# One zero-separated running sum for numerator and denominator, and shared instructions for the first two tiles, in a bidirectional decay scan

## The chip, the cores and the metric

The kernel runs on one core of a Trainium2 chip. The metric is device time in microseconds (us) of one launch. The core has a matrix engine (TensorE, shown as PE, with PEld for its weight loads), a vector engine (VectorE, DVE), a scalar engine for functions such as exp and ln (ScalarE, ACT), a general engine (GpSimd, POOL) and a queue for transfers (SyncE, SP). Each engine works through its own instruction list in order.

## The reference

The input is 32 images of 192 channels and 56 x 56 pixels in float32. Four blocks follow each other, each as `x = x + block(groupnorm(x))`: an attention block, a scan block, a block of shifts, and a long convolution. Only the second is touched. It takes the 3136 pixels of an image as a sequence of tokens, and per channel:

```
k = Wk x;  v = Wv x;  r = Wr x          (192 x 192 products per token)
decay = exp(-exp(w_decay))
p[t+1] = decay * p[t] + exp(k[t]) * v[t]     numerator
q[t+1] = decay * q[t] + exp(k[t])            denominator
y[t]   = (p[t] + exp(u) exp(k[t]) v[t]) / (q[t] + exp(u) exp(k[t]))
x_bi   = 0.5 * (y forwards + y backwards in time)
h      = layernorm over channels( sigmoid(r) * x_bi )
block  = Wo h
```

The reference writes the recurrence with a running maximum; the kernel computes the plain sums above and keeps records by which a guarded version can take over where exponents are large.

## The kernel before, in words

The scan block is `scan_pairs`. It handles two images at a time (16 pairs). A pair is held as three tiles of 128 partitions: tile 0 has channels 0 to 127 of the first image, tile 1 those of the second, tile 2 channels 128 to 191 of both. Time is cut into NM = 4 chunks of MC = 784 tokens, so an operand is 128 x 784. `turned()` gives a PSUM tile of two banks; there are four.

For each chunk there are three pieces of work:

- `forwards(s, m)` (L1170): normalise x on ACT (L1141); for tiles 0 and 1 together, then for tile 2, multiply by Wk, take exp on ACT into `both[:, 1]` (L1183), multiply by Wv, and multiply by the exponential on DVE into `both[:, 0]` (L1188). So `both` holds numerator terms in its first row and denominator terms in its second. Then, per tile, `scan` (L1144) runs one DVE scan per row (L1153), with the carried value `at` as its start and the decay read as a broadcast scalar; POOL puts the carry in the edge column of the result `pq` before (L1150) and takes the new carry from its other end after (L1156); one DVE instruction over 2 x 784 adds the token's own term (L1157). ACT inverts the denominator by Ln and Exp (L1161, L1162), and DVE multiplies into y (L1198).
- `backwards(s, m)` (L1200): the same scan with time reversed over the kept `both`, then the multiply by the inverse (L1220), the addition to the forward y (L1221) and the multiply by the gate g (L1222), where g is a sigmoid in three ACT instructions (L1212 to L1217).
- `finish(s, m)` (L1225): the layer norm and Wo. PE centres (`centre`), ACT squares (L1237), PE averages (`mean_w`), ACT makes the reciprocal deviation `rd` (L1246, L1247), PE multiplies by Wo, and DVE scales from PSUM (L1260) and adds the residual (L1263). ACT's squares for the next norm (L1270) are put off into the following `forwards`.

The loop at L1298 goes through the pairs. For each of the four steps i it emits the first part of `backwards` for chunk 3 - i, the first part of `finish` for the chunk before, then the second parts of both, and then `forwards` for chunk i of the next pair. The next pair's chunk 3 is the last to go forwards and the first to go backwards.

Nobody writes the engines' orders by hand. The program order above sets priorities, and at build time a scheduler places each instruction on its engine's list when its inputs, and a free buffer of its tile's tag, are there by its own reckoning. On the chip the lists are fixed. Buffers: 12 of `both`, 16 of y, 3 of `pq`, 9 of the tag `t` (g, sq, rd), 7 of x.

Of the kernel before, what the change touches and what calls it, by code (L numbers as in the profile page):

```python
# [20 lines left out]
F32 = mybir.dt.float32  # L21
I32 = mybir.dt.int32
AF = mybir.ActivationFunctionType
ALU = mybir.AluOpType
# [12 lines left out]
MC = 784  # L37
NM = N // MC
# [899 lines left out]
def scan_pairs(ctx: ExitStack, tc: tile.TileContext, a, k, x1, st_a, st_c, x2, rs2, count):  # L938
# [5 lines left out]
    nc = tc.nc  # L944
    NB = x1.shape[0]
    cp = ctx.enter_context(tc.tile_pool(name="s_c", bufs=1))
    kp = ctx.enter_context(tc.tile_pool(name="s_k", bufs=3 * NM))
    wp = ctx.enter_context(tc.tile_pool(name="s_w", bufs=9))
    sp = ctx.enter_context(tc.tile_pool(name="s_s", bufs=2))
    pp = ctx.enter_context(tc.tile_pool(name="s_p", bufs=4, space=PSUM))  # L950
    pairs = _Pairs(nc)
# [1 line left out]
    def small(name, shape):  # L953
        return cp.tile(shape, F32, name=name, tag=name)
# [19 lines left out]
    wk, wv, wr = (_blocks_of(weights, 448 * i) for i in range(3))  # L974
# [7 lines left out]
    cb = small("cb", [128, 2])  # L982
    ps, _, _ = turned()
# [15 lines left out]
    eu = small("eu", [128, 2])  # L999
# [31 lines left out]
    def of(t):  # L1031
        return slice(0, 1) if t < 2 else slice(1, 2)
# [93 lines left out]
    class State:  # L1126


        def __init__(self, p):
            self.p = p  # L1130
            self.seen = sp.tile([128, 5, 3 * NM], F32, name="seen", tag="seen", bufs=3)
            self.both, self.y = {}, {}
# [8 lines left out]
            nc.scalar.activation(xs[t], xs[t], AF.Identity, bias=nb1[:, t, s.p : s.p + 1], scale=rs1[:, t, s.p : s.p + 1])  # L1141
        return [parts(t) for t in xs]

    def scan(s, m, t, carry, rev):  # L1144

        both, at = s.both[m][t], carry[t]
        z = wp.tile([128, 2, MC + 1], F32, name="pq", tag="pq", bufs=3)
        edge, last = (MC, 0) if rev else (0, MC)
        out, before = (z[:, :, 0:MC], z[:, :, 1:]) if rev else (z[:, :, 1:], z[:, :, 0:MC])
        nc.gpsimd.tensor_copy(z[:, :, edge], at)  # L1150
        for i in range(2):
            to, data = (out[:, i, ::-1], both[:, i, ::-1]) if rev else (out[:, i], both[:, i])
            nc.vector.tensor_tensor_scan(  # L1153
                to, decay[:, of(t)].to_broadcast([128, MC]), data, at[:, i : i + 1], ALU.mult, ALU.add
            )
        nc.gpsimd.tensor_copy(at, z[:, :, last])  # L1156
        nc.vector.scalar_tensor_tensor(before, both, eu[:, of(t)], before, ALU.mult, ALU.add)  # L1157
        return before[:, 0], before[:, 1]

    def inverse(s, den, m, t, which):  # L1160
        nc.scalar.activation(den, den, AF.Ln)  # L1161
        nc.scalar.activation(den, den, AF.Exp, scale=-1.0, accum_out=s.seen[:, which, 3 * m + t : 3 * m + t + 1])  # L1162

    def start(way):
        carry = [sp.tile([128, 2], F32, name=f"{way}{t}", tag=f"{way}{t}") for t in range(3)]
        for c in carry:
            nc.gpsimd.memset(c, 0.0)  # L1167
        return carry

    def forwards(s, m, behind=()):  # L1170
        s.both[m] = [kp.tile([128, 2, MC], F32, name="both", tag="both") for _ in range(3)]
        s.y[m] = [kp.tile([128, MC], F32, name="y", tag="y", bufs=3 * NM + 4) for _ in range(3)]
        xn = normed(s, m)
        for tiles in ((0, 1), (2,)):
            for wt in (wk, wv):
                ps = [turned() for _ in tiles]
                if len(tiles) == 2:
                    pairs.outer(wt, [q[2] for q in ps], xn)
                else:
                    pairs.inner(wt, ps[0][2], xn)  # L1180
                for t, (_, both, _) in zip(tiles, ps):
                    if wt is wk:
                        nc.scalar.activation(  # L1183
                            s.both[m][t][:, 1].rearrange("p (h n) -> p h n", h=2), both, AF.Exp,
                            accum_out=s.seen[:, 0, 3 * m + t : 3 * m + t + 1],
                        )
                    else:
                        nc.vector.tensor_tensor(  # L1188
                            s.both[m][t][:, 0].rearrange("p (h n) -> p h n", h=2), both,
                            s.both[m][t][:, 1].rearrange("p (h n) -> p h n", h=2), ALU.mult,  # L1190
                        )
                if wt is wk and tiles == (0, 1):
                    for later in behind:
                        later()
            for t in tiles:
                num, den = scan(s, m, t, s.fore, False)
                inverse(s, den, m, t, 1)
                nc.vector.tensor_tensor(s.y[m][t], num, den, ALU.mult)  # L1198

    def backwards(s, m):  # L1200

        xn = normed(s, m)
        h = s.y[m]
        for tiles in ((0, 1), (2,)):
# [5 lines left out]
            for t, (_, both, _) in zip(tiles, ps):  # L1210
                g = wp.tile([128, MC], F32, name="g", tag="t")
                nc.scalar.activation(  # L1212
                    g.rearrange("p (h n) -> p h n", h=2), both, AF.Exp, scale=-1.0,
                    accum_out=s.seen[:, 3, 3 * m + t : 3 * m + t + 1],
                )
                nc.scalar.activation(g, g, AF.Ln, bias=1.0)
                nc.scalar.activation(g, g, AF.Exp, scale=-1.0)  # L1217
                num, den = scan(s, m, t, s.back, True)
                inverse(s, den, m, t, 2)
                nc.vector.tensor_tensor(num, num, den, ALU.mult)  # L1220
                nc.vector.tensor_tensor(h[t], h[t], num, ALU.add)  # L1221
                nc.vector.tensor_tensor(h[t], h[t], g, ALU.mult)  # L1222
            yield

    def finish(s, m):  # L1225

        h, xs = s.y[m], load(s.p, m)
        hs = [parts(t) for t in h]
        sq = [wp.tile([128, MC], F32, name="sq", tag="t") for _ in range(3)]
        for tiles in ((0, 1), (2,)):  # L1230
            ps = [turned() for _ in tiles]
# [4 lines left out]
            for t, (_, both, _) in zip(tiles, ps):  # L1236
                nc.scalar.activation(  # L1237
                    sq[t].rearrange("p (h n) -> p h n", h=2), both, AF.Square,
                    accum_out=s.seen[:, 4, 3 * m + t : 3 * m + t + 1],
# [4 lines left out]
        rds = [wp.tile([128, MC], F32, name="rd", tag="t") for _ in range(3)]  # L1244
# [8 lines left out]
        for tiles in ((0, 1), (2,)):  # L1253
            po = [turned() for _ in tiles]
            if len(tiles) == 2:
                pairs.outer(wog, [q[2] for q in po], hs)
            else:
                pairs.inner(wog, po[0][2], hs)
            for t, (_, out, _) in zip(tiles, po):
                nc.vector.tensor_tensor(  # L1260
                    sq[t].rearrange("p (h n) -> p h n", h=2), out, rds[t].rearrange("p (h n) -> p h n", h=2), ALU.mult
                )
                nc.vector.scalar_tensor_tensor(  # L1263
                    xs[t], sq[t], cb[:, of(t)], xs[t], ALU.add, ALU.add, accum_out=s.sums[:, t, m : m + 1]
                )
                if m == NM - 1:
                    nc.vector.tensor_scalar(s.away[:, t], s.sums[:, t, m : m + 1], -1.0 / MC, None, ALU.mult)

                def square(t=t):
                    nc.scalar.activation(  # L1270
                        sq[t], xs[t], AF.Square, bias=s.away[:, t], accum_out=s.squares[:, t, m : m + 1]
                    )

                left.append(square)
# [20 lines left out]
    s, before = State(0), None  # L1295
    for m in range(NM):
        forwards(s, m)
    for p in range(NP):  # L1298
        ahead = State(p + 1) if p + 1 < NP else None
        for i in range(NM):  # L1300
            m = NM - 1 - i
# [20 lines left out]
        before, s = s, ahead  # L1322
# [20 lines left out]
    ps, _, _ = turned()  # L1343
# [642 lines left out]
```

## Time and profile before

| | us |
|---|---|
| three runs, median (lowest to highest) | 10588.62 (10584.67 to 10590.73) |
| the profiled execution: its time | 10570.28 |
| its span in the profile | 10568.5 |
| DVE busy in the whole span | 9096.0 |
| PE busy in the whole span | 9496.5 |
| ACT busy, POOL busy | 6336.3, 2212.1 |
| granted TensorE clock | 0.96 of full |

The profile's rows name line, engine, operation, output and inputs with the shape of one instruction, how often it ran, its total and mean duration, and the idle time of its engine just before it with what ended it. Mean durations of DVE instructions overlap: the next one starts before the last has ended, so the distance between two starts in the timeline is less than the duration. The four blocks follow one another, and the scan block lies between about 4800 us and 8060 us of the span. In the timeline, the same order of instructions comes back every four chunks, 204.3 us apart.

### The profile page before, as it was taken

Reading aid. Unit: us, or ns where it says so; the run is one execution under the profiler, and the core shown is the slowest. Engines: PE = TensorE matmul, PEld = TensorE weight load, DVE = VectorE, ACT = ScalarE, POOL = GpSimd, SP = SyncE. Lnnn points to the kernel's source line nnn. Section 1 sums busy time; section 2 is a strip of 40 time slices with the busy share of each in tenths; the row PEclk is TensorE's granted clock in tenths of the full one; section 3 lists DMA queues with packets and bytes.
Section 4 is the critical chain, followed back from the end, with each engine's and each line's share of the span. In section 5 each row is a group of like instructions: output and inputs, shape, how many; then the busy total and the mean of one; then the engine's idle time right before and its main releaser. Section 6 shows DMA issues by size and latency. Waiting matters only on the chain. (4 is left out here: it accounts for less than half of the span.)

```text
span 10568.5 us, 164015 instructions
## 1 busy us (share of the span) xinstructions
PE 9496.5 (90%) x64134; PEld 5888.6 (56%) x64134; DVE 9096.0 (86%) x11284; ACT 6336.3 (60%) x11964; POOL 2212.1 (21%) x1750
## 2 busy tenths in 40 slices
PE   5999999999999999998888888888888789999998
PEld 3555555555555655554334433334433677777786
DVE  5888888888888888887999999999999577878787
ACT  3555555555555555554666666666666466767676
POOL 0000000000000000001333333333333444444441
PEclk9999999999999999999899999999999899999999
DMA  4211222112221111102344443444444588989898
GB/s 126 67 53 48 66 67 67 49 52 67 67 67 46 55 48 48 48 27 63 90 102 106 104 99 99 106 102 107 103 99 105 169 271 272 283 274 283 271 279 268
DMA packets 1111104, 1247.70 MB, mean 118 GB/s; under 512 B 773092, under 2 KB 813441, under 8 KB 1098233
## 3 DMA queue, kind: packets, MB, share of 16 engines
q1 hardware_dynamic: 1089388, 1209.08, 39.8%
q10 hardware_dynamic: 20932, 28.02, 1.0%
q8 instruction: 510, 8.36, 0.3%
q14 instruction: 274, 2.24, 0.1%
HBM read 916.15 MB, written 306.43 MB: 116 GB/s over the span
## 5 line engine op out<-in xcount | busy, mean ns | idle before, releaser
L649 DVE SCALAR_TENSOR_TENSOR o<-v_a,att_w,o 128x896 f32<-128x896 f32 (+1 forms) x1024 | 1057.2, 1032 | 421.7 <-ACT v_a L623 301.8
L1167 POOL MEMSET f<- 128x2 f32 x48 | 4.5, 99 | 4744.0 <-DMA st_c<-st 4741.5
L1546 DVE STREAM_TRANSPOSE z<-turned 128x1792 f32<-128x1792 f32 x192 | 677.5, 3529 | 273.2 <-ACT turned L1546 272.9
L1546 ACT COPY y<-ps 64x252 f32<-64x252 f32 (+1 forms) x2304 | 782.1, 339 | 155.1 <-PE ps L1546 125.6
L1161 ACT ACTIVATE pq<-pq 128x784 f32<-128x784 f32 x384 | 329.3, 858 | 679.9 <-DVE pq L1157 679.9
L1153 DVE TENSOR_TENSOR_SCAN pq<-decay,f,both 128x784 f32<-128x784 f32 x384 | 695.5, 1840 | 9.0 <-ACT both L1183 9.0
L1157 DVE SCALAR_TENSOR_TENSOR pq<-both,eu,pq 128x1568 f32<-128x1568 f32 x384 | 701.3, 1840 | 2.0 <-POOL f L1156 0.4
L666 ACT ACTIVATE pr<-ps,low 98x896 f32<-98x896 f32 (+1 forms) x384 | 352.0, 917 | 573.4 <-DVE low L664 573.4
L1153 DVE TENSOR_TENSOR_SCAN pq<-decay,b,both 128x784 f32<-128x784 f32 x384 | 694.1, 1839 | 0.0
L921 PE MATMUL ps<-x,weights 128*128 128x392 f32 x1536 | 587.1, 521 | 93.2 <-ACT x L1141 60.8
L649 DVE SCALAR_TENSOR_TENSOR o<-v_c,att_w,o 128x448 f32<-128x448 f32 (+1 forms) x1024 | 638.6, 624 | 4.8
L662 PE MATMUL ps<-xs_a,gk_a 128*98 128x448 f32 (+1 forms) x1536 | 636.6, 495 | 0.0
L663 PE MATMUL ps<-xs_c,gk_c 125*98 125x448 f32 (+1 forms) x1536 | 631.3, 492 | 0.0
L776 ACT ACTIVATE pq<-pq 128x1176 f32<-128x1176 f32 (+2 forms) x224 | 241.9, 1080 | 640.6 <-DVE pq L768 618.6
L1141 ACT ACTIVATE x<-x,nb,rs 128x784 f32<-128x784 f32 x384 | 386.6, 1030 | 334.3 <-DMA x<-x 178.2
L763 PE MATMUL ps<-gq_a,xs_a 128*128 128x294 f32 (+1 forms) x1600 | 547.0, 425 | 37.8 <-DVE pq L768 33.1
L1546 POOL TENSOR_TENSOR xn<-x,scale 128x896 f32<-128x896 f32 x192 | 334.9, 1744 | 1171.5 <-DMA x<-x 684.2
L1546 PEld LDWEIGHTS ps<-toep,y 128*32 128x32 f32 x16896 | 515.8, 151 | 113.4 <-ACT y L1546 110.6
L1546 PE MATMUL ps<-toep,y 128*32 128x112 f32 x16896 | 563.0, 291 | 0.0
L1156 POOL COPY b<-pq 128x2 f32<-128x2 f32 x192 | 405.4, 2111 | 660.8 <-DVE pq L1153 567.6
L764 PE MATMUL ps<-gq_c,xs_c 125*128 125x294 f32 (+1 forms) x1600 | 520.1, 413 | 0.0
L1546 ACT ACTIVATE turned<-ps,rs 128x448 f32<-128x448 f32 (+1 forms) x576 | 383.3, 666 | 212.8 <-PE ps L1546 206.3
(360 smaller groups left out, 23569.4 us busy)
## 6 DMA issues: line engine op xcount, KB each, us to landing
toep<-spans SPq DMA_DIRECT2D x192, 2352.0 KB
x<-x SPq DMA_DIRECT2D x576, 392.0 KB
x<-x SPq DMA_DIRECT2D x896, 196.0 KB
out_x<-done SPq DMA_DIRECT2D x384, 196.0 KB
spans<-lags SPq DMA_DIRECT2D x24, 2352.0 KB
x<-in_x SPq DMA_DIRECT2D x32, 1568.0 KB
x<-x SPq DMA_DIRECT2D x32, 1568.0 KB
gq_c<-once SPq DMA_DIRECT2D x32, 821.1 KB
```

The lines of the kernel that those rows point to most:

```text
L649: nc.vector.scalar_tensor_tensor(dst, tap(i), dww[:, t, i : i + 1], dst, ALU.mult, ALU.add)
L662: mm(ps[P2, h, :n], g[:, cols], xs_a[j][:, px], start=True, stop=False)
L663: mm(ps[P2, h, :n], gk_c[0:KC, 2 * j + h, cols], xs_c[j][0:KC, px], start=False, stop=True)
L666: nc.scalar.activation(pr[:, :, :n], ps[P2, :, :n], AF.Exp, bias=low[:, j, p : p + 1], accum_out=sums[:, j, p : p + 1])
L763: mm(ps[:m, k - q, :HA], xs_a[j][:, px], g, start=True, stop=False)
L764: mm(ps[:m, k - q, :HA], xs_c[j][0:KC, px], gq_c[0:KC, which[k]], start=False, stop=True)
L921: mm(out, aa, srcs[t][h], start=True, stop=False)
L1141: nc.scalar.activation(xs[t], xs[t], AF.Identity, bias=nb1[:, t, s.p : s.p + 1], scale=rs1[:, t, s.p : s.p + 1])
L1153: nc.vector.tensor_tensor_scan(to, decay[:, of(t)].to_broadcast([128, MC]), data, at[:, i : i + 1], ALU.mult, ALU.add)
L1156: nc.gpsimd.tensor_copy(at, z[:, :, last])
L1157: nc.vector.scalar_tensor_tensor(before, both, eu[:, of(t)], before, ALU.mult, ALU.add)
L1546: return lambda *args, **kw: self.tc.keep_in_program_order(do(*args, **kw))
```

## The change

Only `scan_pairs` is changed. Its edits:

- **One scan per tile.** `both` gets a column in front of each row and one behind the last: numerator and denominator of a tile lie behind each other as [edge, 784, edge, 784, edge]. POOL copies the carries into the edge columns (in front of the rows, or behind them when time is reversed). One DVE scan runs over 2 x 785 elements from 0.0. Its factors come from a new constant `factors`, which is zero at the place of each edge column and the decay elsewhere, so that at an edge the sum restarts from the carry.
- **Sets.** Tiles 0 and 1 become one set that shares `both`, `pq`, the carry, y and g; tile 2 is the other. Own terms (before L1157), Ln and Exp of the denominators, the gate's Ln and Exp, and the DVE products (L1198, L1220 to L1222) are one instruction for both tiles of a set. The scan stays one per tile, and so do the instructions that read PSUM.
- **In-place writes.** Backwards, own terms are added into `both`, not into `pq`; in `finish`, rd is overwritten, not sq.
- **Buffers.** `both`: 4 per set; y: 5 per set; `pq`: 1 per set; g of the first set: 1; tag `t`: 4.
- POOL clears the record `seen` at the start of each pair, since shared instructions leave some of its columns unwritten.

```diff
-    kp = ctx.enter_context(tc.tile_pool(name="s_k", bufs=3 * NM))
-    wp = ctx.enter_context(tc.tile_pool(name="s_w", bufs=9))
+    kp = ctx.enter_context(tc.tile_pool(name="s_k", bufs=NM))
+    wp = ctx.enter_context(tc.tile_pool(name="s_w", bufs=4))
...
+    factors = small("factors", [128, 2, 2 * (MC + 1)])
+    for i in range(2):
+        of_i = factors[:, i].rearrange("p (n c) -> p n c", n=2)
+        nc.vector.memset(of_i[:, :, 0:1], 0.0)
+        nc.vector.tensor_copy(of_i[:, :, 1:], decay[:, i : i + 1].unsqueeze(2).to_broadcast([128, 2, MC]))
...
+    SETS = ((0, 1), (2,))
+
+    def scan(s, m, i, carry, rev):
+
+        both, at = s.both[m][i], carry[i]
+        n, kind = at.shape[1], of(SETS[i][0])
+        z = wp.tile([128, n, MC + 1], F32, name="pq", tag=f"pq{n}", bufs=1)
+        last = 0 if rev else MC
+        nc.gpsimd.tensor_copy(both[:, rev * (MC + 1) :: MC + 1][:, :n], at)
+        for k in range(0, n, 2):
+            to = z[:, k : k + 2].rearrange("p n c -> p (n c)")
+            data = both[:, rev + k * (MC + 1) : rev + (k + 2) * (MC + 1)]
+            if rev:
+                to, data = to[:, ::-1], data[:, ::-1]
+            nc.vector.tensor_tensor_scan(to, factors[:, kind.start], data, 0.0, ALU.mult, ALU.add)
         nc.gpsimd.tensor_copy(at, z[:, :, last])
-        nc.vector.scalar_tensor_tensor(before, both, eu[:, of(t)], before, ALU.mult, ALU.add)
-        return before[:, 0], before[:, 1]
+        own, others = within(both), z[:, :, 1:] if rev else z[:, :, 0:MC]
+        to = own if rev else others
+        nc.vector.scalar_tensor_tensor(to, own, eu[:, kind], others, ALU.mult, ALU.add)
+        return to[:, 0::2], to[:, 1::2]
+
+    def within(both):
+        return both[:, 1:].rearrange("p (n c) -> p n c", c=MC + 1)[:, :, 0:MC]
...
-            for t in tiles:
-                num, den = scan(s, m, t, s.fore, False)
-                inverse(s, den, m, t, 1)
-                nc.vector.tensor_tensor(s.y[m][t], num, den, ALU.mult)
+            num, den = scan(s, m, k, s.fore, False)
+            inverse(s, den, m, k, 1)
+            nc.vector.tensor_tensor(s.y[m][k], num, den, ALU.mult)
...
-                nc.scalar.activation(g, g, AF.Ln, bias=1.0)
-                nc.scalar.activation(g, g, AF.Exp, scale=-1.0)
-                num, den = scan(s, m, t, s.back, True)
-                inverse(s, den, m, t, 2)
-                nc.vector.tensor_tensor(num, num, den, ALU.mult)
-                nc.vector.tensor_tensor(h[t], h[t], num, ALU.add)
-                nc.vector.tensor_tensor(h[t], h[t], g, ALU.mult)
+            nc.scalar.activation(g, g, AF.Ln, bias=1.0)
+            nc.scalar.activation(g, g, AF.Exp, scale=-1.0)
+            num, den = scan(s, m, k, s.back, True)
+            inverse(s, den, m, k, 2)
+            h = s.y[m][k]
+            nc.vector.tensor_tensor(num, num, den, ALU.mult)
+            nc.vector.tensor_tensor(h, h, num, ALU.add)
+            nc.vector.tensor_tensor(h, h, g, ALU.mult)
             yield
```

More of the change, by code (lines that the diff above doesn't have):

```diff
@@ L1131, in __init__ @@
             self.seen = sp.tile([128, 5, 3 * NM], F32, name="seen", tag="seen", bufs=3)
+            nc.gpsimd.memset(self.seen, 0.0)
             self.both, self.y = {}, {}
@@ L1142, in normed @@
         return [parts(t) for t in xs]
[L1144 to L1157, printed above, removed]
-        return before[:, 0], before[:, 1]
@@ L1160, in inverse @@
-    def inverse(s, den, m, t, which):
+    SETS = ((0, 1), (2,))
[11 more added lines that the diff above has]
+            nc.vector.tensor_tensor_scan(to, factors[:, kind.start], data, 0.0, ALU.mult, ALU.add)
+        nc.gpsimd.tensor_copy(at, z[:, :, last])
+        own, others = within(both), z[:, :, 1:] if rev else z[:, :, 0:MC]
+        to = own if rev else others
+        nc.vector.scalar_tensor_tensor(to, own, eu[:, kind], others, ALU.mult, ALU.add)
+        return to[:, 0::2], to[:, 1::2]
@@ L1161, in inverse @@
+    def within(both):
+        return both[:, 1:].rearrange("p (n c) -> p n c", c=MC + 1)[:, :, 0:MC]
+    def inverse(s, den, m, i, which):
         nc.scalar.activation(den, den, AF.Ln)
-        nc.scalar.activation(den, den, AF.Exp, scale=-1.0, accum_out=s.seen[:, which, 3 * m + t : 3 * m + t + 1])
+        at = 3 * m + 2 * i
+        nc.scalar.activation(den, den, AF.Exp, scale=-1.0, accum_out=s.seen[:, which, at : at + 1])
     def start(way):
-        carry = [sp.tile([128, 2], F32, name=f"{way}{t}", tag=f"{way}{t}") for t in range(3)]
+        carry = [sp.tile([128, 2 * len(t)], F32, name=f"{way}{len(t)}", tag=f"{way}{len(t)}") for t in SETS]
@@ L1168, in start, with halved @@
         return carry
+    def halved(t):
+        return t.rearrange("p (h n) -> p h n", h=2)
     def forwards(s, m, behind=()):
-        s.both[m] = [kp.tile([128, 2, MC], F32, name="both", tag="both") for _ in range(3)]
-        s.y[m] = [kp.tile([128, MC], F32, name="y", tag="y", bufs=3 * NM + 4) for _ in range(3)]
+        s.both[m] = [kp.tile([128, 2 * len(t) * (MC + 1) + 1], F32, name="both", tag=f"both{len(t)}") for t in SETS]
+        s.y[m] = [kp.tile([128, len(t), MC], F32, name="y", tag=f"y{len(t)}", bufs=NM + 1) for t in SETS]
         xn = normed(s, m)
-        for tiles in ((0, 1), (2,)):
+        for k, tiles in enumerate(SETS):
             for wt in (wk, wv):
@@ L1180, in forwards @@
                     pairs.inner(wt, ps[0][2], xn)
-                for t, (_, both, _) in zip(tiles, ps):
+                for i, (t, (_, both, _)) in enumerate(zip(tiles, ps)):
+                    bv, ek = (halved(within(s.both[m][k])[:, 2 * i + j]) for j in range(2))
                     if wt is wk:
[L1183 to L1186, printed above, removed]
-                    else:
[L1188 to L1192, printed above, removed]
+                        nc.scalar.activation(ek, both, AF.Exp, accum_out=s.seen[:, 0, 3 * m + t : 3 * m + t + 1])
+                    else:
+                        nc.vector.tensor_tensor(bv, both, ek, ALU.mult)
+                if wt is wk and k == 0:
                     for later in behind:
                         later()
-            for t in tiles:
-                num, den = scan(s, m, t, s.fore, False)
-                inverse(s, den, m, t, 1)
-                nc.vector.tensor_tensor(s.y[m][t], num, den, ALU.mult)
+            num, den = scan(s, m, k, s.fore, False)
+            inverse(s, den, m, k, 1)
+            nc.vector.tensor_tensor(s.y[m][k], num, den, ALU.mult)
     def backwards(s, m):
         xn = normed(s, m)
-        h = s.y[m]
-        for tiles in ((0, 1), (2,)):
+        for k, tiles in enumerate(SETS):
             ps = [turned() for _ in tiles]
@@ L1209, in backwards @@
                 pairs.inner(wr, ps[0][2], xn)
-            for t, (_, both, _) in zip(tiles, ps):
-                g = wp.tile([128, MC], F32, name="g", tag="t")
+            g = wp.tile([128, 2, MC], F32, name="g", tag="g2", bufs=1) if k == 0 else wp.tile([128, 1, MC], F32, name="g", tag="t")
+            for i, (t, (_, both, _)) in enumerate(zip(tiles, ps)):
                 nc.scalar.activation(
-                    g.rearrange("p (h n) -> p h n", h=2), both, AF.Exp, scale=-1.0,
-                    accum_out=s.seen[:, 3, 3 * m + t : 3 * m + t + 1],
-                )
-                nc.scalar.activation(g, g, AF.Ln, bias=1.0)
-                nc.scalar.activation(g, g, AF.Exp, scale=-1.0)
-                num, den = scan(s, m, t, s.back, True)
-                inverse(s, den, m, t, 2)
-                nc.vector.tensor_tensor(num, num, den, ALU.mult)
-                nc.vector.tensor_tensor(h[t], h[t], num, ALU.add)
-                nc.vector.tensor_tensor(h[t], h[t], g, ALU.mult)
+                    halved(g[:, i]), both, AF.Exp, scale=-1.0, accum_out=s.seen[:, 3, 3 * m + t : 3 * m + t + 1]
+                )
+            nc.scalar.activation(g, g, AF.Ln, bias=1.0)
[6 more added lines that the diff above has]
+            nc.vector.tensor_tensor(h, h, g, ALU.mult)
             yield
     def finish(s, m):
-        h, xs = s.y[m], load(s.p, m)
+        h, xs = [t[:, i] for t in s.y[m] for i in range(t.shape[1])], load(s.p, m)
         hs = [parts(t) for t in h]
@@ L1260, in finish @@
                 nc.vector.tensor_tensor(
-                    sq[t].rearrange("p (h n) -> p h n", h=2), out, rds[t].rearrange("p (h n) -> p h n", h=2), ALU.mult
+                    rds[t].rearrange("p (h n) -> p h n", h=2), out, rds[t].rearrange("p (h n) -> p h n", h=2), ALU.mult
                 )
                 nc.vector.scalar_tensor_tensor(
-                    xs[t], sq[t], cb[:, of(t)], xs[t], ALU.add, ALU.add, accum_out=s.sums[:, t, m : m + 1]
+                    xs[t], rds[t], cb[:, of(t)], xs[t], ALU.add, ALU.add, accum_out=s.sums[:, t, m : m + 1]
                 )
@@ L1270, in square @@
                     nc.scalar.activation(
-                        sq[t], xs[t], AF.Square, bias=s.away[:, t], accum_out=s.squares[:, t, m : m + 1]
+                        rds[t], xs[t], AF.Square, bias=s.away[:, t], accum_out=s.squares[:, t, m : m + 1]
                     )
```

## The prediction

> **What bounds the kernel now.** I read the busy time by engine in a stretch of the scan block first, then the waits there, then DVE's timeline through one chunk, then the groups by form. The stretch from 5400 to 7800 us holds 47 chunks (columns: stretch, length, then busy us and instructions of PE, PEld, DVE, ACT, POOL, then clock and transfers):
>
> ```profile
> 5400.00:7800.00 2400.00, 2101.05 (x7652) 950.84 (x7649) 2393.85 (x2243) 1596.15 (x2748) 897.20 (x633) 0.95 0.42 103
> ```
>
> DVE is busy for 2393.85 of 2400 us, PE for 2101 (87.5%). The waits of the same stretch (who <- for whom: us in total, times, longest) name those of PE and a single one of DVE, the last line:
>
> ```profile
> PE ps L921 <- ACT sq L1237: 161.1, 47, 4.4
> ...
> PE ps L924 <- ACT sq L1237: 86.0, 45, 3.7
> ...
> PE ps L921 <- ACT x L1141: 45.5, 31, 1.8
> ...
> DVE pq L1157 <- POOL f L1156: 0.4, 1, 0.4
> ```
>
> So DVE sets the end of every chunk (204.3 us in four, 51.08 us each), and PE waits for ACT, which waits for DVE. Time is won by taking work off DVE, and lost wherever DVE must wait. DVE's timeline from the end of `finish` into `forwards` (start, us, line, tiles), and two PE rows of the same time:
>
> ```profile
> 6006.91 0.96 DVE L1260 TENSOR_TENSOR sq<-ps,rd 128x784 f32<-128x784 f32 x1
> 6007.91 1.03 DVE L1263 SCALAR_TENSOR_TENSOR x<-sq,cb,x 128x784 f32<-128x784 f32 x1
> 6008.87 0.08 DVE L1263 DVE_READ_ACCUMULATOR x<-sq,cb,x 128x1 f32 x1
> 6008.87 3.59 DVE L1153 TENSOR_TENSOR_SCAN pq<-decay,f,both 128x784 f32<-128x784 f32 x2
> 6012.37 1.83 DVE L1188 TENSOR_TENSOR both<-ps,both 128x784 f32<-128x784 f32 x2
> 6014.12 3.58 DVE L1153 TENSOR_TENSOR_SCAN pq<-decay,f,both 128x784 f32<-128x784 f32 x2
> 6017.62 3.59 DVE L1157 SCALAR_TENSOR_TENSOR pq<-both,eu,pq 128x1568 f32<-128x1568 f32 x2
> 6021.12 0.97 DVE L1188 TENSOR_TENSOR both<-ps,both 128x784 f32<-128x784 f32 x1
> ```
>
> ```profile
> 6007.01 2.90 PE L921 MATMUL ps<-x,weights 128*128 128x392 f32 x8
> 6009.84 1.59 PE L924 MATMUL ps<-x,weights 64*128 64x392 f32 x8
> ```
>
> Two things are to be seen. Starts are closer than durations: a scan takes 1.75 us of DVE (6008.87 to 6012.37, halved), not 1.84. And the two scans at 6008.87 come ahead of L1188, which makes the numerator terms: they are the denominators' scans, which need only the exponential. They fill the time in which PE is still multiplying by Wv (the PE rows end at 6011.43).
>
> **What is removed.** A DVE instruction's cost is a rate times elements and a fixed part, and only the fixed part is saved, since every element stays. The own-term instruction L1157 takes 1.75 us for 1568 elements. Its rate, from the same operation of L649 in two sizes (1148 ns for 896, 684 for 448), is 464/448 = 1.036 ns; 1568 of them are 1.624 us, so the fixed part is 0.126 us. The groups by form put both operations side by side:
>
> ```profile
> L1157 DVE SCALAR_TENSOR_TENSOR pq<-both,eu,pq 128x1568 f32<-128x1568 f32 x384 | 701.3, 1840 | 2.0 <-POOL f L1156 0.4
> L1153 DVE TENSOR_TENSOR_SCAN pq<-decay,f,both 128x784 f32<-128x784 f32 x384 | 695.5, 1840 | 9.0 <-ACT both L1183 9.0
> ```
>
> A scan of half the elements has the same mean, 1840 ns. No second size of a scan is in the trace. Its fixed part lies between 0 (all rate; nothing is saved) and 1.75 - 0.81 = 0.94 us (the rate of L1157). I take the equal means at their word: twice the rate, 2.072 ns, and the same 0.126 us. Both ends would need another fixed part with the same total by chance.
>
> - Scans: one of 1570 elements is 3.253 + 0.126 = 3.379 us against 3.50 for two, 0.121 us less. There are 384 pairs (16 image pairs x 4 chunks x 3 tiles x 2 ways): 46.6 us.
> - Own terms: 384 become 256, 128 x 0.126 = 16.1 us.
> - Products L1198, L1220, L1221, L1222: 192 each become 128, 256 in all gone. Start to start they take 0.88 us for 784; the rate, from L780 in two sizes (1377 ns for 1176, 1073 for 882), is 1.034 ns, which leaves 0.07 us: 17.9 us.
>
> Together 81 us off DVE, 1.26 us of each chunk. ACT loses instructions too and POOL four of twelve copies per chunk; neither bounds, so both count nothing.
>
> [...]
>
> **What is added.** Four things.
>
> 1. Building `factors`: two copies of 1568 elements, at most 1.75 us each by L1157's row; none at best, since they stand before the first scan, where DVE still waits for loads. I take 3 us.
>
> 2. Dependent neighbours. Six tile chains become four set chains, so a DVE instruction stands oftener right behind the one whose result it reads. The trace has one such pair, L1260 then L1263 (6006.91 to 6007.91): 1.00 us instead of 0.88. There are between none and eight places per chunk (scan to own term four times, the two backward product chains twice each); 0.13 x 8 x 64 = 67 us at most. Work of the other set lies between at most of them; I take two, 17 us.
>
> 3. The wait for POOL. The scan's input now holds a column that POOL writes. Its own inputs (the carry of the chunk before, a free `both`) are there some 10 us ahead, and POOL is busy 37%, so I count nothing. If that cover goes, DVE stands still meanwhile, and the shortest copy of L1150 took 0.18 us; four times a chunk that is 46 us.
>
> [...]
>
> 4. The wait for the numerators. The single scan needs both rows, so nothing of set 0 can run before L1188. In the rows above `finish` ends at 6008.87 and Wv at 6011.43: 2.56 us that the denominators' scans cover and that now lie open. In the other chunks the distance differs by some tenths at most. What can cover it is the next chunk's backward scan: its terms are kept, its carry is old, and the one `pq` of set 0 is free after the own terms of the backward scan before, since results go into `both`. That fails at the fourth step of a pair, where the next backward chunk is the one that goes forwards: 15 times. Per chunk 0 to 2.56 us over 60 chunks (the first four follow no `finish`): 0 to 154 us. I take half of 15 x 2.56: 19 us.
>
> No transfer is moved, and SP's list stays. The cut buffers cost nothing if each is free before its next use: y of the finished chunk is released by PE before the new one is written, sq by `mean_w` before rd needs the place, `both` by the backward addition, ahead of `finish`. If one is late, it acts through rival B.
>
> **The sum.** -81 + 3 + 17 + 0 + 19 = -42 us. The profiled execution took 10570.28 us (span 10568.5), so 10528 on its footing; the median of the runs is 18.3 us above it, which gives 10547.
>
> **Rivals.**
>
> A, the open numerators: the scheduler does not place a backward scan into the gap, or it isn't ready there. Then DVE waits 2.56 us in 60 chunks: -81 + 3 + 17 + 154 = +93, 10682, slower. It decides from about 1.0 us of open wait per chunk (61/60). For it: the gap is in every chunk, and two short scans stood in it because something had to. Against: L1153 of the backward way already stands ahead of a forward own term at 6027.28, so lists are mixed across pieces.
>
> B, the coarser chain: ACT's Ln of set 0 can start only after two long scans and one long own term, 10.1 us of DVE, where tile 0's started after 5.25: 4.9 us later. ACT works in order, and sq and x, for which PE already waits 292.6 us in 47 chunks (6.2 each), may stand behind it. PE needs 44.7 us of a chunk and has about 5 us to spare in one of 49.8. Where it is late, `finish` and Wv are late too. At 4.9 us in every second chunk on top of A: +93 + 147 = +240, 10829. Against it: if the same Ln is late enough in the scheduler's reckoning, sq goes ahead of it, and PE gains.
>
> C, no change: the scan's fixed part is 0, or two or three of the small waits are paid in part. -81 + 47 + 39 = +5, 10594.
>
> **Chances.** Forecast 0.45 (10500 to 10567: up to all additions at nothing, -81, and a little beyond); C 0.15; A 0.25; B 0.15. 0.2% is 21 us, about what a measurement of this kernel can tell from no change. Faster is the forecast, 0.45; within 0.2% is C, 0.15; slower A and B, 0.40. The range takes in the forecast, C, A and the start of B: 10495 to 10750. The likeliest's own range is 10500 to 10567.
>
> **What would show it.** A scan row of 1570 elements at about 3.47 us mean duration (3.38 start to start), 384 of them; L1157's successor in two forms, the larger at 3.46. DVE still busy above 98% of the stretch and a chunk of about 50.4 us says forecast. DVE idle ahead of the numerators' instruction, released by PE, about 2.5 us a chunk, says A. PE's waits for ACT growing, and DVE idle before the `finish` instructions too, says B. DVE idle released by POOL would show that my cover in the third addition was wrong. A mean scan near 3.68 us says C.

## The result and the profile after

The changed kernel takes 10647.26 us in the median of five runs (10634.14 to 10663.01), beside 10588.62 for the kernel before on the same chip. The ratio is 1.0058, with a 95% interval from 1.0043 to 1.0073: slower by some 60 us, where the likeliest case had said 42 us faster. The forecast failed; the time lies inside the range.

In the profiled execution (10647.26 us, span 10645.5), DVE has less work and more idle time. The stretch from 5400 to 7800 us, with the columns as before (length, then PE, PEld, DVE, ACT and POOL with instructions, clock, transfers):

```profile
5400.00:7800.00 2400.00, 2064.04 (x7472) 925.95 (x7470) 2306.91 (x1641) 1530.20 (x2315) 458.77 (x428) 0.95 0.39 100
```

DVE is busy 2306.91 us of 2400, where it was 2393.85, with 602 instructions fewer. The scan block runs from DVE's first scan at 4926 us to the last record of a pair, at 8209 us before and 8272 us after (not to about 8060, as the part on the time before has it). The waits of DVE from 4925 to 8240 us (who <- for whom: us in total, times, longest) tell for whom it stands idle; the three largest are:

```profile
DVE both L1204 <- PE ps L924: 61.7, 45, 1.6
DVE pq L1164 <- POOL both L1158: 32.0, 120, 0.4
DVE mv L1126 <- ACT rd L1281: 12.8, 14, 0.9
```

Before, DVE waited there for PE once, with the line below, and at the statistics once (0.9 us, at the block's end); no scan waited for POOL.

```profile
DVE both L1188 <- PE ps L924: 2.0, 1, 2.0
```

The scans and the larger own terms, by form (instructions | busy us, mean ns | idle before):

```profile
L1164 DVE TENSOR_TENSOR_SCAN pq<-factors,both 128x1570 f32<-128x1570 f32 x384 | 1303.3, 3419 | 34.1 <-POOL both L1158 32.0
L1168 DVE SCALAR_TENSOR_TENSOR pq<-both,eu,pq 128x3136 f32<-128x3136 f32 x64 | 223.0, 3485 | 2.1
```

And the place that cost most, the end of `finish` and the start of `forwards`, first on DVE, then on PE, then on POOL (start, us, engine, line, tiles, and in brackets the idle time and its releaser):

```profile
6024.61 1.03 DVE L1274 SCALAR_TENSOR_TENSOR x<-rd,cb,x 128x784 f32<-128x784 f32 x1
6025.56 0.09 DVE L1274 DVE_READ_ACCUMULATOR x<-rd,cb,x 128x1 f32 x1
6027.07 1.86 DVE L1204 TENSOR_TENSOR both<-ps,both 128x784 f32<-128x784 f32 x2 [1.42 <-PE ps L924]
6029.22 6.75 DVE L1164 TENSOR_TENSOR_SCAN pq<-factors,both 128x1570 f32<-128x1570 f32 x2 [0.29 <-POOL both L1158]
```

```profile
6023.87 1.58 PE L921 MATMUL ps<-x,weights 128*128 128x392 f32 x4 [0.89 <-DVE rd L1271]
6025.38 1.59 PE L924 MATMUL ps<-x,weights 64*128 64x392 f32 x8
```

```profile
6028.99 0.19 POOL L1158 COPY both<-f 128x4 f32<-128x4 f32 x1 [18.47 <-DVE both L1204]
```

Before, two denominators' scans filled this place for 3.5 us. Now `finish` ends at 6025.65, Wv ends on PE at 6026.97, and DVE stands still for 1.42 us. Then it stands still again: POOL writes the edge columns only after the numerators' products have ended (6028.93), and the scan waits for them.

How the block adds up, from the distance between the starts of DVE's instructions, as a mean over 40 chunks:

| us per chunk | predicted | before | after | difference |
|---|---|---|---|---|
| scans | -0.73 | 21.04 | 20.23 | -0.82 |
| own terms | -0.25 | 10.52 | 10.35 | -0.17 |
| the four products | -0.28 | 10.57 | 10.54 | -0.03 |
| numerators' products L1204 | 0 | 2.63 | 2.78 | +0.15 |
| the rest (`finish`, statistics) | 0 | 6.19 | 6.31 | +0.12 |
| all work of DVE | | 50.96 | 50.21 | -0.76 |
| DVE idle | | 0.13 | 2.05 | +1.92 |
| a chunk | | 51.09 | 52.26 | +1.17 |

1.17 x 64 chunks is 75 us. The block itself, from its first scan to its last record, grew by 64 us (3281.7 to 3346.0), since its first and last chunks differ from the others; the span grew by 77.

### The profile page after: what moved, and what is told of

Read it like the earlier page. It is cut to its first block, busy times and chain, and to the rows that moved or that the text cites. A ratio compares the mean times of both kernels' runs of the same rounds, so it can differ in the third digit from the quotient of the medians.

```text
span 10645.5 us, 161819 instructions
## 1 busy us (share of the span) xinstructions
PE 9497.8 (89%) x64134; PEld 5882.4 (55%) x64134; DVE 9052.0 (85%) x10520; ACT 6308.1 (59%) x11452; POOL 1639.7 (15%) x1478
## 5 line engine op out<-in xcount | busy, mean ns | idle before, releaser
L1164 DVE TENSOR_TENSOR_SCAN pq<-factors,both 128x1570 f32<-128x1570 f32 x384 | 1303.3, 3419 | 34.1 <-POOL both L1158 32.0
L921 PE MATMUL ps<-sq,fixed 128*128 128x392 f32 x512 | 312.3, 782 | 248.8 <-ACT sq L1248 248.8
L1557 PE MATMUL ps<-rows,xn 128*112 128x112 f32 x3072 | 374.2, 279 | 153.9 <-POOL xn L1557 153.8
L921 PEld LDWEIGHTS ps<-x,weights 128*128 128x128 f32 x1536 | 270.2, 192 | 420.1 <-DVE rd L1271 93.5
L1557 PE MATMUL ps<-fixed,padded 128*128 128x168 f32 x3072 | 488.7, 314 | 0.0
L1557 PEld LDWEIGHTS ps<-fixed,padded 128*128 128x128 f32 x3072 | 454.7, 195 | 2.4 <-issue 1.9
```

What stands on the lines that cost most here:

```text
L921: mm(out, aa, srcs[t][h], start=True, stop=False)
L1164: nc.vector.tensor_tensor_scan(to, factors[:, kind.start], data, 0.0, ALU.mult, ALU.add)
L1557: return lambda *args, **kw: self.tc.keep_in_program_order(do(*args, **kw))
```

## The experiments

All ratios are to the kernel before on the same chip, with 95% intervals. e1 to e4, e5 to e8 and e9 to e15 ran on three different chips, so times of different groups are compared by their ratios. Idle time "over the block" is that from 4925 to 8240 us, gaps under 0.15 us included, without the wait of 8 to 13 us at the block's very first chunk; lines of waits are shown as the profile has them. Times per chunk are means over 40 chunks, as in the table. **The theory**, W or W2 in the first expectations and N in the later ones, puts the loss on what the merged scan has to wait for: it needs numerator and denominator, so nothing of a chunk can run on DVE while PE still multiplies by Wv. Its rivals put it on the sets and their longer instructions (S), on the length of the first scan (L), or on the order of the lists (O).

**e1, two scans again, the sets kept.** Own terms and products stay merged.

```
-        nc.gpsimd.tensor_copy(both[:, rev * (MC + 1) :: MC + 1][:, :n], at)
-        for k in range(0, n, 2):
+        nc.gpsimd.tensor_copy(z[:, :, MC if rev else 0], at)
+        for k in range(n):
...
-            nc.vector.tensor_tensor_scan(to, factors[:, kind.start], data, 0.0, ALU.mult, ALU.add)
+            nc.vector.tensor_tensor_scan(to, factors[:, kind.start, 1 : MC + 1], data, at[:, k : k + 1], ALU.mult, ALU.add)
```

> Sets, in-place writes and buffers as changed; only the scan is two again, numerator and denominator each with 784 elements and the carry as its start. Theory W (waits): the loss comes from two waits of DVE in each forward chunk, about 1.3 us for the numerators' products (PE not ready) and about 0.5 us for the POOL copy into both, plus some lost overlap. Here the denominators' scans fill the first and nothing needs the second, so gaps fall from 2.05 us a chunk to under 0.4, scans cost 0.82 us a chunk more: about 10575 us, within 0.3% of before. Theory S (sets): shared, longer instructions and single buffers make ACT and PE late; then the wait for PE stays and the scans come on top: 10690 us or more.

Measured: 10672.03 us, ratio 1.0076 (1.0063 to 1.009). DVE's wait for PE ahead of the numerators is gone, as the theory says, but the time does not come back. The scans' work does (51.16 us a chunk), and another wait stands in the gap. DVE, then ACT:

```profile
6053.09 3.59 DVE L1162 TENSOR_TENSOR_SCAN pq<-factors,f,both 128x784 f32<-128x784 f32 x2 [1.09 <-ACT both L1200]
```

```profile
6051.15 0.95 ACT L1279 ACTIVATE rd<-x,away 128x784 f32<-128x784 f32 x1 [1.63 <-DVE x L1272]
6052.00 0.19 ACT L1279 ACTIVATION_READ_ACCUMULATOR rd<-x,away 128x1 f32 x1
6052.09 0.81 ACT L1200 ACTIVATE both<-ps 128x784 f32<-128x784 f32 x1
```

The denominators' scans wait for their exponentials L1200. These stand on ACT's list behind a put-off square, which waits for DVE's last addition of `finish`. So here the scans that should fill the gap are not ready in it. The expectation (10575 us) had missed this wait. It is not all: of 1.25 us of idle time a chunk it makes 0.55, and much of the rest is gaps under 0.15 us ahead of instructions that read their neighbour's result (0.11 us ahead of L1166 at 6062.03, 0.04 ahead of L1231 at 6041.78).

**e2, early edges.** The forward edge columns are written at the start of `forwards`, ahead of the exponentials and products.

```
+        for both, at in zip(s.both[m], s.fore):
+            edge(both, at, False)
```

> As changed, but in the forward way POOL copies the carries into both as soon as the buffer is there, ahead of the exponentials and products, not behind them. Theory W: DVE's idle time released by POOL (34 us) goes, and the products lose the 0.15 us a chunk of lost overlap: 10600 to 10615 us. Theory S: POOL's copies are not what counts, PE is late anyway and the wait only changes its name: 10640 us or more.

Measured: 10642.54, ratio 1.0056 (1.0041 to 1.007). DVE's idle time ahead of the scans, most of it for POOL, falls from 34.1 to 5.3 us over the block. But the scheduler then lists the backward scan of tile 2 ahead of set 0's own terms in every fourth chunk, and the products wait for ACT's exponential:

```profile
DVE both L1237 <- ACT both L1181: 32.3, 16, 2.1
```

What POOL had cost was paid to ACT; the 10600 to 10615 us expected were not reached. The 61.7 us ahead of the numerators did not move.

**e3 and e4, the whole of `finish` ahead of the second part of `backwards`**, so that tile 2's backward work stands in the gap; e4 adds the early edges.

```
-            next(back)
             left = next(ending) if ending is not None else []
+            next(back)
```

> As changed, but the second part of finish stands ahead of the second part of backwards in program order, so that PSUM is freed for Wk and Wv earlier and tile 2's products stand between finish and the numerators. Theory W: the wait for PE ahead of the numerators' products falls from some 1.1 us a chunk to under 0.4, about 10595 us; the waits for POOL stay. Theory S: the wait for PE stays above 1 us a chunk, 10640 us or more.

> The second and third experiment together. Theory W: both waits go, DVE keeps 0.76 us a chunk less work than before the change: about 10550 us, 0.3 to 0.4% faster than before. Theory S: no better than the change, 10640 us or more.

Measured: 11283.08 (1.0669, 1.0648 to 1.0689) and 11128.78 (1.051, 1.0495 to 1.0524). Some 10595 and 10550 us were expected. They settle nothing about the gap, for they make another bound. In e3, DVE waits 58 times for exponentials (4925 to 8800 us, as its block is longer), and ACT's normalization of x, ahead of them in its list, waits for x to be loaded (5400 to 7800 us):

```profile
DVE both L1204 <- ACT both L1202: 680.8, 58, 13.2
```

```profile
ACT x L1147 <- DMA x<-x: 254.0, 142, 5.5
```

**e5, one scan per tile and nothing else** of the change (results of `finish` in place; no sets).

```
-        for i in range(2):
-            nc.vector.tensor_tensor_scan(
-                to, decay[:, of(t)].to_broadcast([128, MC]), data, at[:, i : i + 1], ALU.mult, ALU.add
-            )
+        nc.vector.tensor_tensor_scan(to, factors[:, of(t).start], data, 0.0, ALU.mult, ALU.add)
```

> The kernel before with only the single zero-separated scan per tile: tiles stay apart in everything else, results stay in pq; rd is written in place and the buffers of t and y are 6 and 15, to make room for the factors. Theory W (the numerators' wait is the loss): work falls 0.82 us a chunk, the open time ahead of the products is some 2.5 us, the POOL copies cost 0.5: about 10720 us. Theory S (the sets are the loss): the waits stay near 1 us, about 10610 us or less.

Measured: 10612.29, ratio 1.0029 (1.0018 to 1.004). Work falls to 50.11 us a chunk. The wait ahead of the numerators is there without any sets, 62.1 us over the block (47.3 of it in the middle stretch); that for POOL is 5.9. The sets are not what opened the gap. The time is that of theory S's expectation, but the wait, 1.4 us in each of 45 chunks, is as long as with the sets; theory W had put it at 2.5. The late edge copies, though, show only with the sets (34.1 us): here tile 0's copy, at 6023.76 us, runs while DVE still multiplies tile 1's numerators (the pair lasts from 6022.72 to 6024.58).

**e6 to e8, fixed orders.** `finish`'s three multiplications ahead of its additions on DVE, so that PSUM comes free sooner, and the put-off squares behind the exponentials of tiles 0 and 1 on ACT. e6 is the changed kernel with this; e7 adds the early edges and pins tile 2's backward scan behind set 0's own terms; e8 is e1 with the two orders.

```
+                after(added, scaled[2])
...
-                        later()
+                        after(later(), exp)
```

> The changed kernel with two orders fixed at build time: on DVE the three multiplications of finish that free PSUM stand ahead of its three additions, on ACT the put-off squares stand behind the exponentials of tiles 0 and 1. No work is changed. Theory W2: PE is late for the numerators because PSUM is freed late and ACT's list holds the exponentials behind work that waits for DVE; then DVE's wait for PE falls from about 62 us to under 25, about 10600 us. Theory S: the sets make the whole chain late, the order of six instructions changes little, 10635 us or more.

> The sixth experiment with the early POOL copies of the second, and with the backward scan of tile 2 fixed behind the own terms of the first set, which the second had moved. Theory W2: gaps fall below 0.6 us a chunk, the work stays 0.8 us a chunk below before: about 10550 us, faster than before by 0.2 to 0.5%. Theory S: 10620 us or more.

> The first experiment (sets kept, two scans per tile) with the two fixed orders of the sixth. Its DVE work was 51.16 us a chunk, 0.2 above before. Theory W2: its wait for the exponentials (1.1 us) goes, about 10605 us; the sets alone then bring nothing, since what instructions save is lost where one stands right behind the one it needs. Theory S: the wait stays, 10650 us or more.

Measured: e6 10695.17 (1.0109, 1.0094 to 1.0124), e7 10585.16 (1.0005, 0.9997 to 1.0014), e8 10633.15 (1.0055, 1.0041 to 1.007). In e6 the wait ahead of the numerators falls to 33.8 us, but the free part of the list shifts again, with the same step as in e2 in 45 chunks:

```profile
DVE both L1235 <- ACT both L1177: 92.4, 45, 2.1
```

With that step pinned and the early edges (e7), the time falls by 110 us, to that of before; 10550 us were expected. 40.3 us ahead of the numerators are left: the fixed orders help, but do not close the gap. e8 differs from e1 by the two orders alone. Its wait for the exponentials goes, but for 8.1 us at the block's start, and yet it is far above the 10605 us expected: 23.9 us of waits for the DMA that brings tile 2's `rd` take its place, and the small gaps stay (from 5400 to 7800 us, 22 of DVE's 49 us of idle time are gaps under 0.15 us). By the ratios it gains 0.2% on e1, with intervals that overlap.

**e9 and e10, one direction each**, on the kernel before: the merged scan backwards alone (e9) and forwards alone (e10).

```
+        if not rev:          # e10: if rev:
...
+            for i in range(2):
+                nc.vector.tensor_tensor_scan(
...
+        else:
```

> The kernel before, with one scan per tile in the backward direction alone; forwards each tile keeps its two scans (no sets, results of finish in place). Theory N (the forward scan over both rows must wait for the numerators, so nothing covers the time in which PE still multiplies by Wv): the denominators' two forward scans stand ahead of the numerators' product again, DVE's wait for PE there is gone (62 us over the block with all scans merged), and three saved scan starts a chunk remain: 3 x 0.13 x 64 = 25 us less than before, ratio 0.9976. Theory S (any merging, by longer instructions, makes PE late): a wait of 30 to 60 us remains, ratio 1.001 to 1.003.

> The opposite half: one scan per tile forwards alone, two per tile backwards. Theory N: the whole wait of about 62 us ahead of the numerators' product stays, less 25 us of saved starts: ratio 1.0035. Theory S: about half the wait, 30 us, ratio 1.0005.

Measured: e9 10604.22 (1.0009, 0.9998 to 1.002), e10 10693.23 (1.0101, 1.0082 to 1.012). Theory N has the place right: e9 waits for PE at no numerators' product at all, e10 at 48, for 89.3 us over the block. Both sizes were wrong. e9's work falls as expected (50.49 us a chunk), but the freed time goes to waits for ACT (8.2 us of the first line lie at the block's start, where the kernel before waits as well):

```profile
DVE pq L1160 <- ACT both L1200: 21.4, 16, 8.2
DVE pq L1237 <- ACT pq L1179: 20.0, 28, 0.8
```

In e10, PE is later than in e5 (the longest wait in the middle stretch is 3.6 us instead of 2.0); it waits for ACT's x (126.8 us there against 33.7). Why ACT's list came out so in e10 was not tried.

**e11, one scan everywhere but for tile 0 forwards**, which keeps two; the condition above reads `if not rev and t == 0:`.

> One scan per tile everywhere but for tile 0 forwards, which keeps two. Theory N: the one denominator scan ahead of the numerators takes 1.75 us and the wait with all scans merged was 1.4 us, so nearly all of it is covered; five saved starts a chunk, 5 x 0.13 x 64 = 42 us, some 5 us of waits for POOL: ratio 0.9965. Theory S: the wait stays, ratio 1.002.

Measured: 10549.55 us, ratio 0.996 (0.9946 to 0.9974), against 0.9965 expected. DVE is busy again throughout, with 210 instructions fewer than before:

```profile
5400.00:7800.00 2400.00, 2102.54 (x7768) 934.97 (x7767) 2392.49 (x2033) 1630.95 (x2787) 1235.15 (x646) 0.97 0.42 104
```

```profile
5999.77 1.84 DVE L1160 TENSOR_TENSOR_SCAN pq<-factors,f,both 128x784 f32<-128x784 f32 x1
6001.53 1.82 DVE L1205 TENSOR_TENSOR both<-ps,both 128x784 f32<-128x784 f32 x2
6003.27 1.83 DVE L1160 TENSOR_TENSOR_SCAN pq<-factors,f,both 128x784 f32<-128x784 f32 x1
6005.12 3.43 DVE L1168 TENSOR_TENSOR_SCAN pq<-factors,both 128x1570 f32<-128x1570 f32 x1
```

One denominator's scan of 1.76 us stands ahead of the numerators, and no idle time follows it. Over the block the wait there is 2.0 us instead of 62.1, and the block in the trace is 55 us shorter than in e5 (3240.9 against 3296.3), from which e11 differs by tile 0's two scans alone. One pair of six left unmerged turns a loss of 0.29% into a gain of 0.4%.

**e12, the changed kernel with tile 0 unmerged forwards**, the orders and early edges of e7.

```
+            if not rev and i == 0 and k == 0:
+                nc.gpsimd.tensor_copy(z[:, 0:2, 0], at[:, 0:2])
+                for j in range(2):
+                    nc.vector.tensor_tensor_scan(
...
+                continue
```

> The changed kernel with fixed orders and early edge copies, as it took the time of before, and two scans for tile 0 forwards. Theory N: the 40 us that it waited for PE ahead of the numerators go, one start a chunk comes back (8 us): ratio 0.9975. Theory S: no gain, ratio 1.001.

Measured: 10537.53, ratio 0.9943 (0.9927 to 0.9959), the fastest median of all, against 0.9975 expected. It differs from e7 (1.0005) by the two scans of tile 0 alone: 1.5 us ahead of the numerators are left of 40.3. It has the changed kernel's buffers, so the smaller numbers of buffers are not the loss. A chunk takes 50.56 us, 0.32 of it idle (2.05 in the changed kernel). At the statistics, where the changed kernel stood idle too, the list now reads:

```profile
6051.27 0.17 DVE L1125 TENSOR_REDUCE mv<-sums 128x3 f32<-128x12 f32 x1
6051.36 1.84 DVE L1164 TENSOR_TENSOR_SCAN pq<-factors,f,both 128x784 f32<-128x784 f32 x1
6053.11 0.14 DVE L1126 TENSOR_REDUCE mv<-squares 128x3 f32<-128x12 f32 x1
```

Here the scan also covers the wait of the statistics for the last square (12.8 us in the changed kernel, now one wait of 0.9 at the block's end, as before): one missing filler had cost at two places. The block is 36 us shorter than before (3245.8 against 3281.7), while the ratio says some 60 for the whole; where the rest lies is open. The profiled execution was the slowest of e12's six, and the untouched blocks behind took 2357 to 2383 us in the traces of all runs. That the sets add anything to e11 is not shown: the two intervals overlap, and e11's chunk is shorter (50.36 us).

**e13 and e14, the same two scans without fixed orders**: e13 with the edges where the change has them, e14 with early edges.

> The changed kernel with two scans for tile 0 forwards and nothing else: the edge columns are still written by POOL behind the numerators, so the denominators' scan, which reads between them, is still listed behind the numerators' product. Theory N (what counts is a scan that can run while PE multiplies by Wv, not how many scans there are): the wait of 62 us for PE stays, one start a chunk is lost (8 us), ratio 1.006 to 1.007. Theory L (it is the length of the first scan that costs): the wait goes, ratio 1.000.

> The same with the forward edge columns written ahead of the exponentials; no order is fixed. Theory N: the denominator's scan stands in the gap, DVE's wait for PE falls from 62 to under 5 us and that for POOL from 32 to about 5; the wait of 32 us for the backward exponential that came with early edges alone may stay: ratio 0.996 without it, 0.999 with it. Theory O (the fixed orders did the work in the kernel that was faster): ratio 1.003 or more.

Measured: e13 10667.08 (1.0077, 1.006 to 1.0094), e14 10601.63 (1.0012, 0.9998 to 1.0027). The pair tells most. e13 has the short scans, but they come behind the numerators and wait there for the edge columns:

```profile
6044.59 1.86 DVE L1212 TENSOR_TENSOR both<-ps,both 128x784 f32<-128x784 f32 x2 [1.42 <-PE ps L924]
6046.74 3.59 DVE L1163 TENSOR_TENSOR_SCAN pq<-factors,f,both 128x784 f32<-128x784 f32 x2 [0.29 <-POOL both L1158]
```

```profile
6046.52 0.19 POOL L1158 COPY both<-f 128x4 f32<-128x4 f32 x1 [18.48 <-DVE both L1212]
```

So the wait is not one of length: 60.2 us ahead of the numerators stay, and theory L falls. In e14 the denominator's scan may go first, and 9.8 us are left of it (under 5 expected). Of the statistics' wait one of 0.9 us at the block's end is left, and 1.6 us for POOL ahead of the scans (about 5 expected). What else remains is the step that e2 opened:

```profile
DVE both L1245 <- ACT both L1189: 35.7, 18, 2.1
```

The ratio is above the 0.999 that was expected with this step. Theory O falls as well: without fixed orders, e14 is 0.46% better than the change (1.0012 against 1.0058). The orders, the one difference from e12, are worth a further 0.7%; the traced blocks differ by 45 us (3290.3 and 3245.8), which fits that step and 8 us ahead of the numerators.

**e15, e12 with the four products per tile.**

```
-            nc.vector.tensor_tensor(s.y[m][k], num, den, ALU.mult)
+            for i in range(len(tiles)):
+                nc.vector.tensor_tensor(s.y[m][k][:, i], num[:, i], den[:, i], ALU.mult)
```

> The fast version (tile 0 with two scans forwards, fixed orders, early edges) with the four products per tile again, 256 more instructions. By the prediction's term, 0.07 us each, it loses 18 us: ratio to before 0.996. By the rows of the changed kernel (10.54 us of products a chunk against 10.57) it loses 2 us: ratio 0.9945.

Measured: 10551.12, ratio 0.9964 (0.9952 to 0.9975). By the ratios the loss is 22 us, nearer the prediction's term, but the interval just overlaps e12's, so the total does not decide between 2 and 18 us. The traces lie near the lower: the products take 10.73 us of a chunk instead of 10.63, idle time falls by 0.06, and the whole chunk has 50.59 us instead of 50.56, 2 us over the block. The two do not agree, and which is right is open.

## Why the prediction was wrong, step by step

**What bounds the kernel** was right, and so was the cover that it named: the denominators' scans fill PE's time on Wv. e5 against e11 and e7 against e12, which differ by the two scans of tile 0 alone, show that it is this that the change loses.

**The scans' saving** was right: 3.371 us start to start for 1570 elements against 3.379 predicted, -52 us against -46.6. Taking the equal means of L1153 and L1157 at their word came out, by luck as much as by reason: no second size of a scan was there to support it. The mean duration is 3419 ns, so case C's 3.68 us did not come about.

**The own terms and products** were sized too large: -11 us against -16.1, and -2 against -17.9. In the merged chain each product reads the one before it, as in these rows of the changed kernel:

```profile
6013.74 1.79 DVE L1232 TENSOR_TENSOR y<-y,both 128x1568 f32<-128x1568 f32 x1
6015.57 1.79 DVE L1233 TENSOR_TENSOR y<-y,g 128x1568 f32<-128x1568 f32 x1
```

A pair of 784 takes 1.76 us start to start where it overlaps, one of 1568 in the chain 1.79 and a gap of 0.04. So these rows show no saving where neighbours depend on each other. That is read from the rows; e15, the one test of it, leaves it open by its total. The second addition had such neighbours, priced at two places a chunk; they stand in every backward chain. (Its 0.13 us are 0.12 by the rows it names, a difference of 2 us.) By the table's first three rows the 768 instructions that went were worth 65 us. Of these, some 10 us go into the numerators' products (+0.15 a chunk) and 8 into the rest (+0.12). **The first addition**, 3 us for `factors`, was 1.77 us for both copies (L1026, 4899.98 to 4901.75).

**The third addition, the wait for POOL at nothing, failed.** I had looked at when the copy's inputs are ready, not at what the copy must stay behind. It writes every 785th column of a tile whose other columns DVE writes; it comes behind them in the program and ran behind them on the chip (at 6028.99 in the rows above, the products ending at 6028.93). In a set it comes behind the products of both tiles, with tiles apart (e5) behind one. The cover of 10 us did not exist, and 34.1 us were paid; my own price "if that cover goes", 46 us, was about right. e2 against the change and e14 against e13, which differ by the place of the copy alone, show it.

**The fourth addition failed, and decided the sign.** It forecast that the next backward scan covers the gap but for 15 of 60 chunks. It covers it in none: the schedule places that scan after the numerators' own terms, and 45 chunks wait 1.37 us for PE. In 14 others the statistics stand in the gap, with the wait of 0.9 us of their own. That is rival A by its mechanism, at 62 us instead of 154. The gap was mis-sized with it: Wv ends 9.7 us after `finish` begins, where it was 10.85 before, so 1.3 to 1.4 us lie open and not 2.56. In the chunks shown PE has two waits for `finish`'s multiplications, 1.16 and 0.89 us, to free PSUM, where it had one of 1.76 us for ACT's x (at 6003.98 in the trace of before). The savings were smaller too, so the sign turned at this smaller price: about 50 us of work saved against 62 here, 34 for POOL and 13 at the statistics.

**Rival B** was wrong: in the rows above, what PE waits for just ahead of DVE's idle time is DVE's `rd` (L1271), not ACT. The statistics' 12.8 us stood in none of the cases.

Added up, over the block from its first scan to its last record: 52 us less work, where 81 were predicted, and 116 us more idle time, where the additions came to 39. Of the 116, 60 lie ahead of the numerators, 34 ahead of the scans, 13 at the statistics, about 7 in gaps under 0.15 us ahead of dependent neighbours, and the rest in single waits. That is +64 us against -42, 106 apart; 100 lie between 10547 and 10647. What stays open: why the schedule does not use the backward scan (no run forced the next chunk's scan into the gap), and what moved ACT's list in e10.

## What to carry to other kernels

An instruction that merges two can take over the waits of both, as the merged scan did here (61.7 us ahead of the numerators, where it was 2.0): ask what the earlier of the two was covering, and keep one unmerged at the place where something has to run while another engine finishes (e11, e12: one pair in six). When an engine has no idle time, price a merge by start-to-start distances of dependent neighbours (here 1.83 us for one product of 1568 elements in the chain, 1.76 for two of 784), not by the fixed cost per instruction. A small helper copy into a tile that another engine is writing came behind that writing here, for 34.1 us of idle time ahead of the scans; put it ahead of it in the program, and look at what the lists become then (e2, e14).

## What was unexpected in the hardware

In e13 a POOL copy of four columns into the edges takes 0.19 us while DVE is idle (L1158 at 6046.52, shown above). Another of four columns, from `pq` to the carry, takes 3.44 us beside an own-term instruction on DVE of 3.49 us (DVE, then POOL):

```profile
6001.43 3.49 DVE L1176 SCALAR_TENSOR_TENSOR pq<-both,eu,pq 128x3136 f32<-128x3136 f32 x1
```

```profile
6001.52 3.44 POOL L1173 COPY f<-pq 128x4 f32<-128x4 f32 x1 [7.08 <-DVE pq L1172]
```

In the trace of the change, the copies of four columns to the carry (L1165) take 0.85 us beside a product of 0.95 us (L1210, 59 times) and 3.43 to 3.44 us beside own terms of 3.48 us (L1168, 60 times), and end 0.05 us after that instruction. The copies of four columns into the edges (L1158) take 0.19 us where DVE is idle (63 times). But 109 copies of two columns to the carry take 0.19 us beside own terms of 1.86 us. So a copy was not long beside every instruction of DVE, and what makes it long no run shows. It cost little here: no wait of DVE names the copy back to the carry. ACT's Ln does wait for it (L1175, 394.6 us in 59 waits), but there the copy ends within 0.05 us of the own terms, which Ln needs as well.

The second thing: where a product on DVE read its neighbour's result, it started only when that had wholly ended (above, L1232 ends at 6015.53 and L1233 starts at 6015.57; in the trace of the change the start lies 0.03 to 0.04 us behind the end in all 118 places where L1231 and L1232, or L1232 and L1233, of 1568 elements stand side by side). Independent neighbours started before the end: two scans of 784 by 0.08 to 0.11 us (L1153 in the trace of before, 290 places), and products of 0.97 us stand 0.88 us apart there.
